# Expert blocks of a mixture of experts: one pass for a wide block and a block of 32 rows together, each piece of code once behind a branch

## Chip, core and metric

One core of a Trainium2 chip runs the whole kernel in one launch. The metric is the time of one execution in microseconds of the device; of several executions, the median.

## What is computed

A graph network's two attention layers, then one transformer block whose feed-forward part is a mixture of experts, on 625 rows of 768 numbers, all in float32. The change touches the last part alone:

```python
h2 = _ln(x, ln2_g, ln2_b).reshape(-1, d)              # 625 x 768
gate_logits = h2 @ Wg                                 # 8 experts
w, sel = jax.lax.top_k(gate_logits, 1)
...
hid = jax.nn.relu(jnp.einsum('nd,edf->enf', h2, W1) + b1[:, None, :])   # 768 -> 3072
y = jnp.einsum('enf,efd->end', hid, W2) + b2[:, None, :]                # 3072 -> 768
return x + moe.reshape(b, t, d)      # each row takes the y of its one expert
```

With one expert per row the softmax weight is 1, so a row's result is its sum `x` plus its expert's `y`. The experts' loads are uneven: the reference's gate sends 293, 152, 82, 57, 36 and 5 rows to six of them and none to two.

## The kernel before

Engines: PE (TensorE) multiplies, DVE (VectorE) and ACT (ScalarE) work on tiles, POOL (GpSimd) issues transfers by computed rows, SP (SyncE) issues all other transfers. Each engine runs its own queue in order. Inside the expert stage the orders of PE and of SP are written out by hand; a scheduler places the instructions of the others.

**Rows.** After the gate, each tile of 125 rows is scattered to HBM by expert, `xg` for the normalised rows and `xr` for the sums with the row's number behind them (`send`, `send_sums`, L998 to L1013). An expert has 640 places in both. Places that no row took hold a number beyond the last row, and a scatter to `out` leaves those out.

**The first expert.** The expert that has most of the first 125 rows is taken up while the other rows are still on their way: up to 128 of its rows are one pass ahead of the loop (`step_a`). Beside it DVE works out a table for the rest.

**The table** (L1330 to L1417). The rows left of each expert are cut into blocks of 128 rows, a block of 64 and a block of 32; each block is one pass of the loop, smaller blocks first. Each entry has the block's kind, its first row, its expert, whether the next pass's expert is a new one, and the same of the pass after that. `SHUFFLE` orders the experts by rank.

**One pass** (`step`, L1163 to L1275) holds the hidden rows as they come from the matmul, with rows on partitions:
- `into(c)` multiplies the turned rows `xbT` by a chunk of W1 into PSUM (L1186) and DVE copies it out (`hb`, L1190). With 64 or 32 rows, two or four chunks of columns share the array side by side.
- `turn(c)` transposes 128x128 pieces of `hb` on the PE (L1197), and ACT adds b1 and applies the relu on the way out (L1203).
- `out_of(c)` multiplies these by W2 into `py` (L1212).
- At the end DVE adds b2 and the row's sum (L1259, L1268), and POOL scatters the rows to `out` (L1270).

Within a pass, chunks of `into` and `out_of` follow closely. `turn_rows` (L905) transposes the next pass's rows `xb` on the PE in the last two chunks, and ACT copies them to `xbT`. POOL loads `xb` (L1456) and the sums `rb` (L1136), both 128 rows or less at 3 KB a row, and waits for what a pass before left in those tiles.

**Weights.** W1 and W2 of one expert fill six pieces in SBUF, three of 3 MB each. SP refills a piece for the next expert as soon as the last matmul that reads it is done (`load_expert`, L1144), each piece in two halves. The third piece of W1 has a copy ahead: `load_ahead` fills two spare tiles with that of the expert after next, and ACT copies them into place in each pass (`from_ahead`, L1161).

**The loop** (L1450 to L1470) reads the table entry on every engine and branches to one of three bodies, each a whole `step` with its loads:

```python
with tc.If(kind == 0) as cmp:
    part(B)
with cmp.Else():
    with tc.If(kind == 1) as cmp2:
        part(64)
    with cmp2.Else():
        part(32)
```

Of the kernel before, what the change touches and what calls it, by code (L numbers as in the profile page):

```python
# [20 lines left out]
N = 625  # L21
# [21 lines left out]
NS = E * 2 + N // B  # L43
SHUFFLE = (0, 3, 1, 4, 2, 5, 6, 7)
TA = 3
RE = 640
NR = E * RE + B
# [3 lines left out]
BH = E * NK // 2  # L51
NEG = -1.0e30
# [10 lines left out]
def gnn_moe_kernel(ctx: ExitStack, tc: tile.TileContext, p, out):  # L63
# [630 lines left out]
    with tc.tile_pool(name="att", bufs=1, reuse_waits="tile") as a1, \  # L694
# [210 lines left out]
        def turn_rows(dst, src, ps, part, copy):  # L905

            k0, k1 = ((0, 4), (4, KD))[part]
            tp = ps.tile([128, 512], F32, tag="tp", name="tpx").rearrange("p (k r) -> p k r", k=4)
            for k in range(k0, k1):
                nc.tensor.transpose(tp[:, k - k0, :], src[:, k * 128:(k + 1) * 128], ident)  # L910
            return copy(dst[:, k0:k1, :], tp[:, :k1 - k0, :])
# [86 lines left out]
        def send(t):  # L998

            pk = ps.tile([128, 512], F32, tag="tp", name="pk")  # L1000
            for s in range(t + 1):
# [5 lines left out]
                                           op0=OP.mult, op1=OP.add, accum_out=slot)  # L1007
            nc.vector.scalar_tensor_tensor(pos[t], ef[:, t:t + 1], float(RE), slot, op0=OP.mult,
# [70 lines left out]
        nc.gpsimd.dma_start(xa, xg[ds(first_e * RE, B), :])  # L1079
# [6 lines left out]
        nc.gpsimd.dma_start(ra, xr[ds(first_e * RE, B), :])  # L1086
# [17 lines left out]
    def load_half(to, e, c, k, **cond):  # L1104
        nc.sync.dma_start(to, W1[ds(e, 1), k * 128:(k + 3) * 128, c * FC:(c + 1) * FC]
                          .rearrange("o (k p) f -> p (o k) f", p=128), **cond)

    def load_piece(e, l, c, **cond):
        if l:
# [4 lines left out]
            for i in range(2):  # L1114
                nc.sync.dma_start(to[i], of_e[i], **cond)  # L1115
# [9 lines left out]
    ps = ctx.enter_context(tc.tile_pool(name="rps", bufs=1, space=PSUM, reuse_waits="tile"))  # L1125
    sp = ctx.enter_context(tc.tile_pool(name="sps", bufs=2, space=PSUM, reuse_waits="tile"))
    piece(ewa, 0, 0)
# [6 lines left out]
    def sums_so_far(row, M):  # L1134
        rb = mw.tile([B, D + 1], F32, name="rb", bufs=1)
        nc.gpsimd.dma_start(rb[:M], xr[ds(row, M), :])  # L1136
        return rb
# [6 lines left out]
    def load_expert(e, new, later, last=NFC - 1):  # L1144


        with tc.manual_schedule(engines={SP}):
            for c in range(last):
                load_piece(e, 0, c, cond=new)
            load_bias(e, cond=new)  # L1150
            load_piece(e, 1, 0, cond=new)
            load_ahead(*later)
            for c in range(1, NFC):
                load_piece(e, 1, c, cond=new)

    def load_ahead(e, new=None):
        for i in range(2):
            load_half(ahead[i], e, NFC - 1, 3 * i, **({} if new is None else dict(cond=new)))

    def from_ahead(i):  # L1160
        nc.scalar.copy(w1[NFC - 1][:, 3 * i:3 * i + 3, :], ahead[i])  # L1161

    def step(M, xT, bT, rb, after=None):  # L1163

        P = B // M
        C = 512 if P == 1 else FC // P
        n = DF // (C * P)
        K = C // 128  # L1170
        py = [sp.tile([128, 512], F32, name=f"py{i}", bufs=1) for i in range(2)]
        hb, hbT, copied = {}, {}, []

        def block(c, g, k):

            return 2 * k + c % 2 if P == 1 else g * K + k

        def into(c):
# [5 lines left out]
            for k in range(KD):  # L1184
                for g in range(P):
                    mm = nc.tensor.matmul(  # L1186
                        ph[g * M:(g + 1) * M, :C].rearrange("p (j f) -> p j f", f=128),
                        xT[:, k, :M], w[:, k, g], start=(k == 0), stop=(k == KD - 1))
            hb[c] = mw.tile([128, 512], F32, name="hb")
            copied.append(nc.vector.tensor_copy(hb[c][:, :C], ph[:, :C]))  # L1190
            return mm

        def turn(c):

            tp = sp.tile([128, 4, 128], F32, tag="tp", name="tph")
            for k in range(K):
                nc.tensor.transpose(tp[:, k, :], hb[c][:, k * 128:(k + 1) * 128], ident)  # L1197
            hbT[c] = mw.tile([128, 4, 128], F32, name="hbT", bufs=6)
            for k in range(K):
                for g in range(P):  # L1200
                    f = block(c, g, k) + (c // 2 if P == 1 else c) * (FC // 128)
                    r = slice(g * M, (g + 1) * M)
                    nc.scalar.activation(hbT[c][:, k, r], tp[:, k, r], AF.Relu, bias=bT[:, f:f + 1])  # L1203

        def out_of(c):
            w = w2[c // 2 if P == 1 else c]

            order = [(k, i) for k in sorted(range(K), key=lambda k: block(c, 0, k) % 2)
                     for i in range(2)]
            for k, i in sorted(order, key=lambda o: o[1]) if c == n - 1 else order:  # L1210
                for g in range(P):
                    mm = nc.tensor.matmul(  # L1212
                        py[i][g * M:(g + 1) * M, :384], hbT[c][:, k, g * M:(g + 1) * M],
                        w[:, block(c, g, k), i * 384:(i + 1) * 384],
# [3 lines left out]
        with tc.manual_schedule(engines={PE}):  # L1218
            into(0)
            begun = into(1)  # L1220
        yield begun
        if after is None:
            with tc.manual_schedule(engines={PE}):
                turn(0)
                turn(1)
                yield out_of(0)
        with tc.manual_schedule(engines={PE}):
            if after is None:
                into(2)
                into(3)  # L1230
                turn(2)
                out_of(1)
                for c in range(2, n):
                    if c + 2 < n:
                        into(c + 2)
                    else:
# [265 lines left out]
```

## Time and profile before

| what | us |
|---|---|
| median of three runs (lowest, highest) | 1045.74 (1045.42, 1046.21) |
| the profiled execution, its own time | 1046.59 |
| its span, first to last instruction | 1045.0 |
| PE's first matmul in the loop, and the end of its last | 689.72, 1032.89 |
| one chunk of `into` or `out_of`: 128 rows, 64 rows, 32 rows | 5.15, 5.31, 2.73 |
| transposes of hidden rows per chunk: 128, 64, 32 rows | 0.44, 0.59, 0.37 |
| transposes of the next rows, two parts in a pass: 128 rows | 0.44 + 0.22 |
| the same, 64 or 32 rows | 0.44 + 0.37 |
| from 700 to 1045: PE, DVE, ACT busy, of 345 | 318.2, 55.8, 103.7 |
| one copy of `from_ahead` on ACT | 2.75 |
| DVE's copy of 128x512 out of PSUM, of 128x256 | 0.69, 0.43 |
| load of 32 sums from issue to landing, median; the shortest load of sums, in the first pass | 5.4, 3.5 |
| scatter to `out` from issue to landing: median; the last one | 5.6, 2.3 |

How to read it: "busy" counts an instruction's time on its engine. A line of the timeline gives start, length, engine, line of the source, operation, what it writes and reads with shapes (a matmul 128*64 has 64 rows), how many instructions were merged, and in brackets the idle time before them with what ended it. Each float32 matmul shows as two. In a line of stretches the last three figures are the granted clock of the PE (1.00 is full), the busy share of the 16 transfer engines and GB/s. "T" will be used for the end of a pass on the PE.

### The profile page before, as it was taken

To read this page: it belongs to the slowest core of one execution; us is meant where nothing else is said; L and a number is where in the kernel's file an instruction comes from. 1 tells how busy PE (TensorE), PEld (TensorE's weight loads), DVE (VectorE), ACT (ScalarE), POOL (GpSimd) and SP (SyncE) were. 2 spreads that over 40 slices of the span, in tenths; PEclk is the share of its full clock that TensorE was granted. 3 is DMA by queue.
4 is the path that set the end of the run, shared out by engine and by line. 5 is a ranking of instruction groups with operands and counts; after the bars stand their busy time and mean duration, and the time that the engine had idled before them with its cause. 6 is when DMAs were issued, how large, how long until landed. Compare 5 with 4: busy or idle time off the path is not lost. (4 is left out here: it accounts for less than half of the span.)

```text
span 1045.0 us, 14928 instructions
## 1 busy us (share of the span) xinstructions
PE 984.0 (94%) x4733; PEld 568.7 (54%) x4734; DVE 449.4 (43%) x1337; ACT 355.6 (34%) x791; POOL 57.0 (5%) x97
## 2 busy tenths in 40 slices
PE   6889999999999999999999899998999899999893
PEld 4455456677555556677776555543454344634241
DVE  7877697285375740475545545011101121011212
ACT  6667554263140120444442201113131243134232
POOL 1200100000000010000000112000000000000000
PEclk9999999999999999999999889999999999999997
DMA  9300400300230173999300778333759977899893
GB/s 287 137 1 2 163 31 0 136 1 1 74 77 1 46 182 70 392 383 353 132 1 1 276 259 317 122 118 135 267 220 393 404 292 263 319 397 399 313 403 131
DMA packets 86197, 195.93 MB, mean 187 GB/s; under 512 B 32429, under 2 KB 34100, under 8 KB 86137
## 3 DMA queue, kind: packets, MB, share of 16 engines
q1 hardware_dynamic: 80617, 177.14, 47.2%
q0 software_dynamic: 5440, 17.86, 5.1%
q8 instruction: 34, 0.56, 0.2%
q14 instruction: 26, 0.21, 0.1%
q10 hardware_dynamic: 80, 0.16, 0.1%
HBM read 253.45 MB, written 38.37 MB: 279 GB/s over the span
## 5 line engine op out<-in xcount | busy, mean ns | idle before, releaser
L1212 PE MATMUL py<-ew,hbT 128*64 128x384 f32 (+2 forms) x960 | 187.8, 498 | 6.8 <-DMA ew<-in_L_ffn_W_dram 6.8
L1186 PE MATMUL ph<-ew,xbT 128*32 128x256 f32 (+2 forms) x864 | 155.2, 498 | 9.3 <-issue 4.8
L1212 PEld LDWEIGHTS py<-ew,hbT 128*64 128x64 f32 (+2 forms) x960 | 88.9, 145 | 85.6 <-issue 51.0
L1203 ACT ACTIVATE hbT<-tph,bT 128x64 f32<-128x64 f32 (+2 forms) x240 | 55.2, 333 | 229.5 <-PE tph L1197 162.6
L1186 PEld LDWEIGHTS ph<-ew,xbT 128*32 128x32 f32 (+2 forms) x864 | 62.1, 136 | 92.3 <-issue 84.6
L1268 DVE TENSOR_TENSOR yo<-yo,py 64x192 f32<-64x192 f32 (+2 forms) x80 | 27.6, 378 | 158.5 <-PE py L1212 157.7
L1190 DVE COPY hb<-ph 128x512 f32<-128x512 f32 (+1 forms) x39 | 24.4, 629 | 159.9 <-PE ph L1186 159.9
L530 PE MATMUL agg<-xl,zT 125*125 125x256 f32 (+1 forms) x300 | 79.8, 417 | 1.3 <-ACT zT L519 1.1
L530 PEld LDWEIGHTS agg<-xl,zT 125*125 125x125 f32 x300 | 54.5, 188 | 19.6 <-ACT zT L519 2.6
L357 PE MATMUL pp<-w,yT 128*125 128x512 f32 x120 | 56.1, 607 | 0.0
L232 ACT ACTIVATE step<-iota,past 125x314 f16<-125x314 f16 x120 | 55.9, 549 | 0.0
L630 PE MATMUL ph<-wr,h1T 128*125 128x384 f32 x160 | 52.8, 486 | 0.0
L592 PE MATMUL ph<-w,h1T 128*125 128x384 f32 x160 | 52.4, 486 | 0.0
L249 PE MATMUL cps<-step,oh 125*125 125x314 f16 x181 | 37.1, 307 | 10.5 <-ACT step L232 5.4
L854 DVE CUSTOM_DVE_ANT_0 e<-sc,later 125x625 f32<-125x625 f32 (+4 forms) x60 | 29.8, 542 | 36.2 <-PE sc L838 36.2
L858 ACT ACTIVATE e<-e,of 125x625 f32<-125x625 f32 (+4 forms) x60 | 35.7, 596 | 23.3 <-DVE of L854 23.3
L920 PE MATMUL po<-wpj,aT 128*125 128x384 f32 x120 | 42.8, 504 | 0.4 <-DVE xx L924 0.4
L167 PE MATMUL ph<-wr,yT 128*125 128x512 f32 x96 | 42.1, 593 | 0.1
L242 DVE TENSOR_SCALAR oh<-iota,drel,upper 125x125 f16<-125x125 f16 x160 | 41.1, 315 | 2.3 <-PE cps L249 2.2
L592 PEld LDWEIGHTS ph<-w,h1T 128*125 128x125 f32 x160 | 30.0, 188 | 21.2 <-issue 0.5
L630 PEld LDWEIGHTS ph<-wr,h1T 128*125 128x125 f32 x160 | 29.8, 188 | 20.8
L772 PE MATMUL pv<-L_ffn_Wv,hT 128*125 128x384 f32 x120 | 39.5, 486 | 0.0
(337 smaller groups left out, 1253.6 us busy)
## 6 DMA issues: line engine op xcount, KB each, us to landing
ew<-in_L_ffn_W_dram SPq DMA_DIRECT2D x114, 1536.0 KB
xr<-zt SPq DMA_DIRECT2D x5, 3076.0 KB
xg<-zt SPq DMA_DIRECT2D x5, 3072.0 KB
ahead<-in_L_ffn_W_dram SPq DMA_DIRECT2D x10, 1536.0 KB
xid<-in_L_ffn_W_dram SPq DMA_DIRECT2D x10, 1536.0 KB
w<-in_L_gnn_W_dram SPq DMA_DIRECT2D x4, 1536.0 KB
wr<-in_L_gnn_Wr_dram SPq DMA_DIRECT2D x4, 1536.0 KB
b2b<-in_L_ffn_b_dram SPq DMA_DIRECT2D x11, 384.0 KB
```

Of the source, the lines that this page charges most:

```text
L167: nc.tensor.matmul(pp[:R, :], yT[:, c, cols(t)], part(wr1, KD, c, i, 512), start=(c == 0), stop=(c == KD - 1))
L232: nc.scalar.activation(o, iota[:, :SH + 1], AF.Sign, bias=at, scale=-1.0)
L242: m = nc.vector.tensor_scalar(o, iota[:, :n], at, weight, op0=OP.is_equal, op1=OP.mult)
L357: nc.tensor.matmul(pp[:R, :], yT[:, c, cols(t)], part(w1, KD, c, i, 512), start=(c == 0), stop=(c == KD - 1))
L530: nc.tensor.matmul(self.agg[:R, c0:c0 + n], zT[:, s, :], xl[:, s, x0:x0 + n], start=(s == 0), stop=(s == T - 1))
L592: nc.tensor.matmul(ph[:R, :384], h1T[:, c, cols(t)], part(w2, KH, c, i, 384), start=(c == 0), stop=(c == KH - 1))
L630: nc.tensor.matmul(ph[:R, :384], h1T[:, k, cols(t)], part(wr2, KH, k, i, 384), start=(k == 0), stop=(k == KH - 1))
L772: nc.tensor.matmul(pp[:R, :384], hT[:, c, cols(t)], w[i][:, c, :], start=(c == 0), stop=(c == KD - 1))
L920: nc.tensor.matmul(po[t, i][:R, :384], aT[:, c, cols(t)], wpj[i][:, c, :], start=(c == 0), stop=(c == KD - 1))
L1186: mm = nc.tensor.matmul(ph[g * M:(g + 1) * M, :C].rearrange("p (j f) -> p j f", f=128), xT[:, k, :M], w[:, k, g], start=(k == 0), stop=(k ...
L1203: nc.scalar.activation(hbT[c][:, k, r], tp[:, k, r], AF.Relu, bias=bT[:, f:f + 1])
L1212: mm = nc.tensor.matmul(py[i][g * M:(g + 1) * M, :384], hbT[c][:, k, g * M:(g + 1) * M], w[:, block(c, g, k), i * 384:(i + 1) * 384], star ...
```

## The change

**Passes.** A pass now takes at most one wide block (128 or 64 rows) and one block of 32, of the same expert; an expert with 160 rows left has one pass of 128+32. The entry has three bits for the pieces, the expert, the new flag and the same of the next pass. Rows for a pass are read as one run of 160 places, the block of 32 first; so each expert's places begin 32 later in `xg` and `xr`. The order of experts changes (`SHUFFLE`).

**Order in a pass.** All `into` chunks and part of the turns of the wide block (`begin`), then the narrow block as a whole, then the rest of the wide block (`end`). W1 for the next expert is asked for after the narrow block's first matmuls (or after `begin`), W2 after `end`. The copy of W1 ahead is gone.

**Transposes.** DVE turns the next rows in blocks of 32x32 with one instruction. For this POOL loads `xb` as four quarters of the columns, 32 partitions each, 160 rows in runs of 192 numbers, and W1 lies in SBUF with rows 6p to 6p+5 of it on partition p. `xb` and its turned form take the place of `xid`, so the first expert's rows are still turned on the PE. The narrow block's hidden rows are turned by DVE too, straight from PSUM, and ACT applies bias and relu in place; its matmuls read W1 in runs of 32 columns.

**Scatters.** Each pass sends both: the wide block's rows, then the narrow block's. A block that a pass does not have has all its row numbers set beyond the last row.

The core of the diff:

```diff
-NS = E * 2 + N // B
-SHUFFLE = (0, 3, 1, 4, 2, 5, 6, 7)
+NS = E + N // B
+SHUFFLE = (0, 3, 2, 4, 1, 5, 6, 7)
+Q = 32
+U = B // Q + 1
...
+            nc.vector.tensor_scalar_add(slot, slot, float(Q))
...
-        nc.sync.dma_start(to, W1[ds(e, 1), k * 128:(k + 3) * 128, c * FC:(c + 1) * FC]
-                          .rearrange("o (k p) f -> p (o k) f", p=128), **cond)
+        nc.sync.dma_start(to, W1[ds(e, 1), :, c * FC:(c + 1) * FC]
+                          .rearrange("o (p k) f -> p (o k) f", p=128)[:, k:k + 3], **cond)
...
-    def load_ahead(e, new=None):
-        for i in range(2):
-            load_half(ahead[i], e, NFC - 1, 3 * i, **({} if new is None else dict(cond=new)))
-
-    def from_ahead(i):
-        nc.scalar.copy(w1[NFC - 1][:, 3 * i:3 * i + 3, :], ahead[i])
...
+    def load_first(e, new):
+        with tc.manual_schedule(engines={SP}):
+            for c in range(NFC):
+                load_piece(e, 0, c, cond=new)
+
+    def load_second(e, new):
+        with tc.manual_schedule(engines={SP}):
+            load_bias(e, cond=new)
+            for c in range(NFC):
+                load_piece(e, 1, c, cond=new)
...
+        def begin(self):
+            self.into(0)
+            self.into(1)
+            for c in range(2, self.n):
+                self.turn(c - 2)
+                mm = self.into(c)
+            return mm
+
+        def end(self):
+            n = self.n
+            self.out_of(0)
+            self.turn(n - 2)
+            self.turn(n - 1)
+            for c in range(1, n):
+                mm = self.out_of(c)
+            return mm
+
+    def prepare(rows, idx, M):
+        nc.vector.tensor_copy(idx[:M], rows.bitcast(I32)[:M, D:D + 1])
+        nc.vector.tensor_add(rows[:M, :D], rows[:M, :D], b2b[:M])
...
+    w1b = ewb.tile([128, 2, KD, FC], F32, name="w1b")
+    w1[1:] = [w1b[:, i] for i in range(2)]
...
+    def rows_in(row):
+        rows = xg[ds(row, U * Q), :].rearrange("(b r) (q c) -> q r b c", r=Q, q=4)
+        for q in range(4):
+            nc.gpsimd.dma_start(xb[q * Q:(q + 1) * Q], rows[q])
+
+    def turn_next():
+        return nc.vector.transpose(xT.rearrange("p j (b r) -> p b j r", r=Q),
+                                   xb.rearrange("p b (r j) -> p b j r", r=Q))
...
+    def narrow(bT, *then):
+        def into(c, n, w):
+            ph = sp.tile([128, 512], F32, name="ph")
+            v = ph[:, :n * BLK * Q].rearrange("p (c j r) -> p c j r", c=n, r=Q)
+            for k in range(KD):
+                for g in range(4):
+                    nc.tensor.matmul(v[g * Q:(g + 1) * Q], xT[:, k, :Q], w[:, :, k, :, g],
+                                     start=(k == 0), stop=(k == KD - 1))
+            to = hq[:, c * BLK:(c + n) * BLK]
+            nc.vector.transpose(to, ph[:, :n * BLK * Q].rearrange("p (j r) -> p j r", r=Q))
+            for j in range(c * BLK, (c + n) * BLK):
+                nc.scalar.activation(hq[:, j, :], hq[:, j, :], AF.Relu, bias=bT[:, j:j + 1])
...
+            into(0, 1, w1[0][:, None].rearrange("p c k (j g r) -> p c k j g r", g=4, r=Q))
+            into(1, 2, w1b.rearrange("p c k (j g r) -> p c k j g r", g=4, r=Q))
+        load_first(*then)
...
+                        nc.tensor.matmul(
+                            pq[i][g * Q:(g + 1) * Q, :384], hq[:, c * BLK + j + g, :],
...
+        prepare(rq, iq, Q)
+        add_up(rq, pq, Q)
...
+        rows_in(row_next)
+        nc.gpsimd.dma_start(rw, xr[ds(row + Q, B), :])
+        nc.gpsimd.dma_start(rq, xr[ds(row, Q), :])
+        bT, s = biases((w >> 8) & 7)
...
+        with tc.If((w & 2) == 2) as c64:
+            with tc.manual_schedule(engines={PE}):
+                of[64].begin()
+        with c64.Else():
+            with tc.If((w & 4) == 4):
+                with tc.manual_schedule(engines={PE}):
+                    of[B].begin()
+        with tc.If((w & 1) == 1) as c32:
+            narrow(bT, *then)
+        with c32.Else():
+            nc.vector.memset(iq, N)
+            load_first(*then)
+        turn_next()
+
+        def finish(M):
+            if M < B:
+                nc.vector.memset(iw[M:], N)
+            prepare(rw, iw, M)
+            with tc.manual_schedule(engines={PE}):
+                of[M].end()
+            load_second(*then)
+            add_up(rw, pw, M)
+
+        with tc.If((w & 2) == 2) as d64:
+            finish(64)
+        with d64.Else():
+            with tc.If((w & 4) == 4) as d128:
+                finish(B)
+            with d128.Else():
+                load_second(*then)
+                nc.vector.memset(iw, N)
+        for rows, idx, M, after in ((rw, iw, B, first_made), (rq, iq, Q, first_load)):
+            s = scatter_out(rows, idx, M)
+            tc.add_manual_dep(s.ins, after.ins.name, ORDER)
```

`rq`, `iq`, `pq` and `hq` are the narrow block's sums, row numbers, results in PSUM and hidden rows; `rw`, `iw` and `pw` the wide block's. `add_up` adds the results in PSUM to the sums as the old lines L1262 to L1268 did; `Wide.into`, `turn` and `out_of` do what the old functions of these names did.

## The prediction

> **What bounds the kernel now.** I read the page first, then its stretches, then the PE's work in order of time over the expert stage, last the queue of POOL.
>
> ```profile
> span 1045.0 us, 14928 instructions
> ...
> PE 984.0 (94%) x4733; PEld 568.7 (54%) x4734; DVE 449.4 (43%) x1337; ACT 355.6 (34%) x791; POOL 57.0 (5%) x97
> ```
>
> TensorE bounds the span. The change lies in the loop over experts, from 689.7 us on, and in how it is entered. The PE's matmuls there, some of them (start, length, what they are, idle time before):
>
> ```profile
> 727.12 11.98 PE L1186 MATMUL ph<-ew,xbT 128*128 128x512 f32 x24 [3.07 <-DVE bT L1142]
> ...
> 833.02 6.75 PE L1186 MATMUL ph<-ew,xbT 128*32 128x256 f32 x96 [4.82 <-issue]
> ...
> 852.50 10.57 PE L1186 MATMUL ph<-ew,xbT 128*128 128x512 f32 x24
> ...
> 917.85 10.52 PE L1186 MATMUL ph<-ew,xbT 128*64 128x512 f32 x48
> ...
> 952.10 5.39 PE L1186 MATMUL ph<-ew,xbT 128*32 128x256 f32 x96
> ...
> 971.35 3.12 PE L1212 MATMUL py<-ew,hbT 128*32 128x384 f32 x24 [2.91 <-DMA ew<-in_L_ffn_W_dram]
> 974.39 11.19 PE L1186 MATMUL ph<-ew,xbT 128*64 128x512 f32 x48
> ...
> 1009.32 5.39 PE L1186 MATMUL ph<-ew,xbT 128*32 128x256 f32 x96
> ...
> 1029.58 3.31 PE L1212 MATMUL py<-ew,hbT 128*32 128x384 f32 x24 [2.99 <-DMA ew<-in_L_ffn_W_dram]
> ```
>
> The reader is to see nine passes, of 64, 128, 64, 32, 128, 64, 32, 64 and 32 rows, and that most begin without a gap. An undisturbed pass takes 917.85 - 852.50 = 65.35 us (128 rows) or 952.10 - 917.85 = 34.25 (64); one of 32 is 18.2 from its pieces in the table above. Two 128, four 64 and three 32 make 322.3; the PE works until 1032.9, 343.2 after 689.7. The other 20.9: **first visits** to the body for 128 rows (3.07, and 11.98 - 10.57 = 1.4 at a lower clock) and for 32 rows (4.82, and 6.75 - 5.39), together 10.7; **weights** that came late in the seventh and ninth pass (22.3 and 23.6 us instead of 18.2, and 0.7 at 974.39), together 10.2.
>
> **The change, part by part.**
>
> *Passes.* By the new table the same blocks make seven passes: 64 | 128 | 64 | 64+32 | 64 | 128+32 | 32. The matmuls that stream weights stay. Gone from the PE: the rows' turn (0.81 in the four passes of 64 and the three of 32, 0.66 in the two of 128, 0.66 in the first pass), 7.7; the turn of the hidden rows in the blocks of 32, three of 0.37 each in three blocks, 3.3. **-11.0.** VectorE takes them: a turn of 960 columns, by the copy of 512 at 691 ns some 1.3 us, in a stage where it is busy 56 of 345 us. The PE does not wait for it before the next pass: it stands behind the first matmuls and has 17 us (64 rows) or more of second matmuls as cover. The new 32-row matmuls read W1 in runs of 32 columns, not 128; no row shows that: bounds 0 and, were they twice as slow, three times 8.1 us. I take 0, since the old pass of 128 rows reads W1 in runs of 128 columns and that of 64 in one run of 512, and their matmuls take 605 and 600 ns. ScalarE loses eighteen copies of 2.75 us that ended no wait.
>
> *First visits.* The old loop has one body for each width; the new one has five pieces (start 64, start 128, narrow, end 64, end 128) in the order in which they run. Of the old bodies the first cost what the loop's entry shows in both; the other two cost 10.7. Bounds: all hidden (-10.7), or four new pieces at 5.3 each (+10.7). I take **0**. The row that bears on it: the last packet of the instruction queue lies at 828 us, and the five later jumps between bodies (852, 917, 952, 974, 1009) leave no gap.
>
> [...]
>
> *Weights.* The rows of 3 MB read ahead go; instead the first matmuls of a pass all end before its second ones, so that W1 of the next expert can be loaded during the second half, and W2 during the next first half. The queue carries about 400 GB/s when full:
>
> ```profile
> 940.00:950.00 10.00, 10.00 (x64) 4.76 (x64) 0.34 (x2) 2.59 (x10) 0.00 (x0) 1.00 1.03 405
> ```
>
> So 3.95 us per half piece of 1.57 MB, 48.5 for an expert with its bias, and about 4 for the rows, sums and results of a pass (1.4 MB, much of it now in runs of 768 bytes). From the start of the third pass the queue is full: 8 (the last W2 of its own expert), two experts 97, one pass's rows three times 12, the first W1 piece of the sixth pass 8 and 1.5 to land: 126.5. The PE wants it after 33.5 + 49.8 + 33.5, with 2.6 of slack and about 3 of a first visit: 122.4. It waits 4, some 5 with the piece behind it, and no longer in the last pass: 5 - 10.2 = **-5**. Bounds: -10.2 (rows cost 2.5) and +8 (rows 6, halves 4.2). If a chain of transfers this full slips, every us is the PE's.
>
> *A new wait in the last pass.* In the build's order of instructions VectorE's first two in the narrow piece are the index copy and the addition of b2 to rq (942 ns in the old row for 32 rows), both behind the load of rq; the turns of the narrow hidden rows are queued behind them, ScalarE's relus behind these, and the PE's second matmuls behind those. The load of rq is the last of POOL's six loads, and POOL now sends two scatters per pass, the second only when the first has landed. POOL's rows (start, length), a 128-row pass that ended on the PE at 793.96, and the last:
>
> ```profile
> 795.66 1.02 POOL L1270 DMA_INDIRECT out_dram<-yo,idx  x1 [64.50 <-DVE yo L1268]
> 798.84 0.58 POOL L1456 DMA_DIRECT2D xb<-xg  x1 [2.15 <-PE ph L1186]
> 800.06 0.54 POOL L1136 DMA_DIRECT2D rb<-xr  x1 [0.65 <-issue]
> ...
> 1036.79 0.92 POOL L1270 DMA_INDIRECT out_dram<-yo,idx  x1 [19.94 <-DVE yo L1268]
> ```
>
> and the time from issue to landing, medians, last in each line:
>
> ```profile
> rb<-xr POOLq DMA_DIRECT2D x3, 96.1 KB, 5.4
> out_dram<-yo,idx POOLq DMA_INDIRECT x10, 5.6
> ```
>
> With T the end of a pass on the PE: first scatter T+1.7, landed T+7.3, second scatter out T+8.3, first rows 2.15 later, T+10.5; four issues of 0.57 with gaps of 0.65 to T+15.4; rw to T+16.6; rq landed between 3.5 (its shortest, quiet queue) and 5.4 later, T+21. Then 0.14 + 0.94, the turn of 256 columns 0.43, a relu 0.30: the PE goes on at T+22.8. In the pass 64+32 its first matmuls end at T+24.4, in 128+32 far later: hidden. In the last pass, 32 rows alone, they end at T+8.1: 14.7 lost, of which a slower landing or gaps could make 18 and faster ones 10. A low clock after it (3.31 us for the last 24 matmuls) is inside that spread. **+15.**
>
> *The end.* After VectorE's last addition there stand now, before the scatter that counts: the turn for a pass that does not come (1.3), two branches and a memset (0.5, the old loop's turn-round of 1.4 at most), and the wide scatter, all of it out of bounds, which must land first: 0.97 (its issue) to 5.6; the shortest in the old trace, the quiet last one, took 2.3, to which I hold. With a little for the second hand-over, **+4.5**, bounds 2.5 to 8.
>
> [...]
>
> *Small ones, at nothing:* one more addition on 125x1 per tile; the order in which the first expert's W2[1] and W1[2] are released swaps, so W1[2] lands by my count near 654 to 656 and its halves are wanted at 655.3 and 657.9 (bounds 0, +2).
>
> Sum: -11.0 + 0 - 5 + 15 + 4.5 = +3.5, on the profiled execution's 1046.6 (span 1045.0 and 1.6 around it) 1050.1. That execution lies 0.85 above the median of the runs, so **1049** on their scale. A measurement of this kernel can tell about 0.2%, 2.1 us, from no change.
>
> **Rivals.**
> (a) *Faster: the code is found ready.* The five pieces lie in order of execution, so that fetching ahead may cover their first visits. Then -10.7: 1038. For it: the old gaps follow jumps backward or over a body. Against: the 4.82 has no visible cause. It decides from 5.5 us of the 10.7 saved.
> (b) *Faster: the last pass waits little*, since POOL's queue turns faster than its old rows: at a wait of 3 us, 1037. Against: each step is a row.
> (c) *Slower still: the full queue.* Row packets or the new address order of W1 cost more: halves at 4.2 and rows at 6 make the +8 above, 13 more than forecast: 1062.
> (d) *The terms cancel* to within 2.1 us.
> (e) *Every jump stalls:* two in each of seven passes at the 3.07 us of 727.12 are 43 us: 1092. Against: the five jumps without a gap.
>
> **Chances.** Forecast, 1047.9 to 1056: 0.34; (c) 0.12; (e) 0.03; so slower 0.49. (a) 0.21 and (b) 0.14: faster 0.35. (d) 0.16. The range 1036 to 1063 takes in all but the ends of (b), (c) and (e); the forecast's own is 1048 to 1056.
>
> **What will show it.** Right: no transposes on the PE in the loop but those of the wide blocks; seven passes; in the last, an idle PE of 10 to 18 us between first and second matmuls that VectorE's rq addition ends; two scatters at the end, 2 to 6 us apart; waits for weights only about the sixth pass. Wrong: gaps at every branch, DMA below 380 GB/s in the full stretch, or a last pass without the wait.

## The result, and the profile after

The changed kernel took 1053.41 us (median of four runs, 1051.67 to 1054.71) against 1045.58 of the kernel before in the same runs: ratio 1.0075, 95% interval 1.0058 to 1.0093. The forecast was 1049, slower, within 1036 to 1063, a range that also takes in faster times. The sign held, and so did the narrower range of the forecast itself, 1048 to 1056; the loss, 7.8, is more than twice the 3.3 forecast. The profiled execution took 1053.03 us, 6.44 more than that of before. The head of its page:

```profile
span 1049.5 us, 14689 instructions
...
PE 974.1 (93%) x4511; PEld 597.8 (57%) x4512; DVE 462.8 (44%) x1347; ACT 301.0 (29%) x753; POOL 78.4 (7%) x129
```

TensorE is busy 9.9 us less than before (984.0), and the time is longer all the same: what was taken off the engine that bounds the kernel came back as time in which it stands still. PE's matmuls in the loop at three of the six seams, at the waits for weights and in the last pass (start, length, what they are, idle time before; PEq and DVEq are the queue of an engine, its branches and waits, and not the engine itself):

```profile
708.27 5.49 PE L1213 MATMUL pw<-ew,hT 128*64 128x384 f32 x32 [0.68 <-PEq L1513]
...
759.49 5.40 PE L1213 MATMUL pw<-ew,hT 128*128 128x384 f32 x16 [1.01 <-DVE hb L1190]
...
843.13 2.80 PE L1460 MATMUL ph<-ew,xid 128*32 128x256 f32 x48 [1.02 <-DVE hb L1190]
...
909.53 4.09 PE L1213 MATMUL pw<-ew,hT 128*64 128x384 f32 x24 [1.83 <-DMA ew<-in_L_ffn_W_dram]
...
917.21 7.96 PE L1187 MATMUL ph<-ew,xid 128*128 128x512 f32 x18 [0.82 <-DMA ew<-in_L_ffn_W_dram]
...
962.51 2.98 PE L1476 MATMUL pq<-ew,hq 128*32 128x384 f32 x30 [0.30 <-DMA ew<-in_L_ffn_W_dram]
...
1000.64 4.36 PE L1460 MATMUL ph<-ew,xid 128*32 128x256 f32 x48 [3.11 <-DVEq L1510]
1004.81 5.34 PE L1460 MATMUL ph<-w1b,xid 128*32 128x512 f32 x48
1018.70 11.00 PE L1476 MATMUL pq<-ew,hq 128*32 128x384 f32 x96 [8.55 <-issue]
```

The first matmul of the second to the sixth pass does not wait. There are three kinds of gaps: one of 0.7 to 1.0 us inside every pass with a wide block, at the seam between its two halves; three short waits for weights about the sixth pass; and two long ones in the last pass. The label "issue" of the longest says only that the profile saw no single releaser. VectorE's rows of the same time show what it was (start, length, operation, idle time before):

```profile
1016.63 0.14 DVE L1238 COPY iq<-rq 32x1 int32<-32x1 int32 x1 [17.08 <-DMA rq<-xr]
1016.86 0.94 DVE L1239 TENSOR_TENSOR rq<-rq,b2b 32x768 f32<-32x768 f32 x1
1017.73 1.03 DVE L1463 STREAM_TRANSPOSE hq<-ph 128x256 f32<-128x256 f32 x2
```

VectorE stood 17.08 us at the load of rq, and the turns of the hidden rows, whose input was there from 1005 on, were queued behind it, as forecast. GpSimd's rows about that time and at the end:

```profile
999.25 1.05 POOL L1254 DMA_INDIRECT out_dram<-rw,iw  x1 [68.98 <-DVE rw L1250]
1006.54 0.90 POOL L1254 DMA_INDIRECT out_dram<-rq,iq  x1 [6.24 <-DMA out_dram<-rw,iw]
1009.73 2.65 POOL L1435 DMA_DIRECT2D xid<-xg  x4 [2.29 <-issue]
...
1013.66 0.54 POOL L1501 DMA_DIRECT2D rq<-xr  x1 [0.40 <-issue]
1036.04 1.05 POOL L1254 DMA_INDIRECT out_dram<-rw,iw  x1 [21.84 <-DVE iw L1536]
1039.04 0.90 POOL L1254 DMA_INDIRECT out_dram<-rq,iq  x1 [1.96 <-DMA out_dram<-rw,iw]
```

The second scatter waits 6.24 for the first one's landing, and the load of rq is the last of six: it went out 16.1 after TensorE had ended its pass at 997.5. The stretches of 10 us show the clock (last three figures: granted clock, busy share of the transfer engines, GB/s):

```profile
1000.00:1010.00 10.00, 9.36 (x96) 3.87 (x96) 0.00 (x0) 0.00 (x0) 1.47 (x3) 0.83 0.92 361
1010.00:1020.00 10.00, 1.45 (x13) 1.18 (x13) 2.04 (x4) 1.72 (x9) 3.23 (x6) 0.70 0.32 100
1020.00:1030.00 10.00, 9.70 (x93) 8.46 (x85) 1.48 (x3) 3.48 (x17) 0.00 (x0) 0.78 0.00 0
```

The clock was half for 3.4 us from 1000.4 and for 10.2 us from 1014.1. The first matmuls of the pass took 4.36 instead of 2.80, the last ones 11.00 instead of 8.52: 4.0 us more behind gaps of 11.7.

From the two profiled executions, the difference by its parts:

| part | how | forecast | measured |
|---|---|---|---|
| matmuls and turns themselves | 338.5 from 691.18 to 1029.70, less the 24.8 of gaps and low clock below = 313.7; before 322.3 | -11.0 | -8.6 |
| first visits, seams | the 10.7 of before are gone; six seams: 0.84, 1.01, 0.82, 1.75, 0.81, 0.98 = 6.2 | 0 | -4.5 |
| waits for weights | 1.83 + 0.82 + 0.30 = 2.95; before 10.2 | -5 | -7.2 |
| the last pass | 8.55 + 3.11 + clock 4.0 | +15 | +15.7 |
| from TensorE's end to the span's | 19.8 (1029.7 to 1049.5); before 12.1 (1032.9 to 1045.0) | +4.5 | +7.7 |
| the loop's start | 691.18; before 689.72 | 0 | +1.5 |
| outside the span | 3.53; before 1.59 | none | +1.9 |
| sum | | +3.5 | +6.4 |

### The profile page after: what moved, and what is told of

It reads as the page before. It is cut to its first block, busy times and chain, and to the rows that moved or that the text cites. A ratio compares the mean times of both kernels' runs of the same rounds, so it can differ in the third digit from the quotient of the medians.

```text
span 1049.5 us, 14689 instructions
## 1 busy us (share of the span) xinstructions
PE 974.1 (93%) x4511; PEld 597.8 (57%) x4512; DVE 462.8 (44%) x1347; ACT 301.0 (29%) x753; POOL 78.4 (7%) x129
## 5 line engine op out<-in xcount | busy, mean ns | idle before, releaser
L1213 PE MATMUL pw<-ew,hT 128*64 128x384 f32 (+1 forms) x672 | 159.8, 487 | 5.5 <-PEq L1513 2.0
L1213 PEld LDWEIGHTS pw<-ew,hT 128*64 128x64 f32 (+1 forms) x672 | 101.4, 160 | 58.3 <-issue 14.1
L1203 ACT ACTIVATE hT<-tph,bT 128x64 f32<-128x64 f32 (+1 forms) x168 | 41.0, 361 | 282.6 <-PE tph L1198 188.5
L1187 PE MATMUL ph<-w1b,xid 128*64 128x512 f32 (+1 forms) x288 | 85.7, 594 | 0.0
L1190 DVE COPY hb<-ph 128x512 f32<-128x512 f32 x30 | 20.7, 691 | 142.0 <-PE ph L1187 142.0
L1187 PEld LDWEIGHTS ph<-w1b,xid 128*64 128x64 f32 (+1 forms) x288 | 34.5, 155 | 41.5 <-issue 37.7
L1250 DVE TENSOR_TENSOR rw<-rw,pw 64x192 f32<-64x192 f32 (+1 forms) x48 | 12.9, 315 | 92.5 <-PE pw L1213 92.3
L1187 PE MATMUL ph<-ew,xid 128*64 128x512 f32 (+1 forms) x144 | 43.1, 595 | 1.8 <-SPq L1493 1.0
```

The source lines that it names most:

```text
L1187: mm = nc.tensor.matmul(ph[g * M:(g + 1) * M, :C].rearrange("p (j f) -> p j f", f=128), self.xT[:, k, :], w[:, k, g], start=(k == 0), stop ...
L1203: self.made = nc.scalar.activation(hT[c][:, k, r], tp[:, k, r], AF.Relu, bias=self.bT[:, f:f + 1])
L1213: mm = nc.tensor.matmul(pw[i][g * M:(g + 1) * M, :384], hT[c][:, k, g * M:(g + 1) * M], w[:, self.block(c, g, k), i * 384:(i + 1) * 384], ...
```

## The experiments

Three theories were at stake. For the last pass: VectorE's queue at rq's load, set by GpSimd's queue, or else the weights. For the seams: the hand-over of the last copy, the skipped branch, or code that has to be fetched. For the end: the second scatter, or something behind it. Single runs of one kernel lie up to 10 us apart here (1039.2 to 1049.4 of the kernel before), while its medians were 1044.5 to 1045.6 in the groups of runs; so ratios are compared, and single gaps in the traces.

**1. The work on rq behind the turns.**

```diff
-        prepare(rq, iq, Q)
+        with tc.issue_after(turned.ins):      # the last turn of the hidden rows
+            prepare(rq, iq, Q)
         add_up(rq, pq, Q)
```

> The changed kernel with one thing moved: in the narrow block VectorE turns the hidden rows first, and only then copies rq's row numbers and adds b2. Theory (VectorE's queue): the 8.55 us that TensorE idles in the last pass between first and second matmuls are VectorE standing at the load of rq (landed at 1016.6) with the turns queued behind it. Then the idle time falls to about 1 us (a turn 0.43, a relu 0.32, hand-overs), and the half clock that followed it (second matmuls 11.0 us instead of 8.5) goes as well: 8.55 - 1 + 2.5 = 10 less, 1043. Rival (weights): TensorE waits for W2, whose last pieces were on their way until about 1008; then the idle time stays near 8 and the time at 1053. Rival (the wait moves): the additions of the results wait for rq instead, at the end of the pass; they start at about 1021 and rq lands at 1016.6, so I expect nothing of it.

Measured 1042.82, ratio 0.9963 (0.9944 to 0.9981). The wait is gone:

```profile
1000.89 4.49 PE L1460 MATMUL ph<-ew,xid 128*32 128x256 f32 x48 [3.10 <-DVEq L1512]
1005.17 5.36 PE L1460 MATMUL ph<-w1b,xid 128*32 128x512 f32 x48
1010.32 7.95 PE L1477 MATMUL pq<-ew,hq 128*32 128x384 f32 x96
```

VectorE still waited for rq, until 1017.06, but with nothing behind it that TensorE needs. The queue theory holds with its size, 10.6 of forecast 10. This one order of two instructions is more than the whole loss: without it the change makes the kernel faster by 0.4%.

**2. The scatters independent of each other.**

```diff
+        tc.declare_no_dep(both[1].ins, both[0].ins, reason="other rows")
```

> The changed kernel with the two scatters of a pass declared to touch different rows, so that the second does not wait until the first has landed; the scatter of the narrow rows then stands ahead of the wide one in GpSimd's queue. Theory (GpSimd's queue sets when rq is loaded): in the pass before the last, 6.24 us of waiting for a landing and an issue of 0.9 go from in front of the last pass's loads, so rq lands 7 us earlier, TensorE's idle time falls from 8.55 to about 1.5 and the half clock after it mostly goes (-2.5); at the end the second scatter no longer waits 1.96 for the first, -3. Together 12 less: 1041. Rival (the load of rq is bound by the weights in the transfer queues): it lands no earlier, only the end gains: 1050.5.

Measured 1047.60, ratio 1.0014 (0.9991 to 1.0036): between the two. GpSimd asked for rq at 1007.91, 5.7 earlier, but its transfer, as the view of transfers shows (last column: us from issue to landing), took 7.2; in the changed kernel it took 2.9:

```profile
rq<-xr POOLq DMA_DIRECT2D x1, 96.1 KB, 7.2
```

```profile
rq<-xr POOLq DMA_DIRECT2D x1, 96.1 KB, 2.9
```

The weights' transfers were under way until 1015.5 here (1010.4 in the changed kernel), and rq's rows shared the transfer engines with them, which were 90% busy or more until 1012. So rq landed only 1.4 earlier: GpSimd's queue bounds the load in the changed kernel, and once that queue is shorter the transfers do. The wait fell from 8.55 to 6.42, and the way from the last addition to the end of the span by 3.0.

**3. The seam filled with 5 us of matmuls.**

```diff
                 mm = self.into(c)
+            self.out_of(0)
             return mm
         def end(self):
             n = self.n
-            self.out_of(0)
```

> The changed kernel with the first chunk of second matmuls (5 us on TensorE) moved from behind the seam between the two halves of a wide block to ahead of it; nothing else changes. Theory (hand-over): the gaps of 0.66 to 1.02 at the six seams are TensorE waiting for VectorE's last copy out of PSUM (0.69) and for the branches, with nothing queued; with 5 us of matmuls that need neither, five or six of them go, 4.5 to 6 less in all: 1048. Rival (the jump itself costs: code has to be fetched): a gap stays at each seam, the time stays within 1 us of 1053.4.

Measured 1054.07, ratio 1.0076 (1.0052 to 1.0100): nothing gained. In the four passes without a narrow block the gap moved along with the seam, and behind it came a second one, since the turns now stand first there. The third pass:

```profile
815.50 1.06 PE L1198 MATMUL tph<-ident,hb 128*128 128x128 f32 x8 [0.69 <-PEq L1513]
816.97 10.64 PE L1213 MATMUL pw<-ew,hT 128*64 128x384 f32 x64 [0.41 <-ACT hT L1203]
```

So there it is not the copy. In the two passes with a narrow block, where the branch is taken, the gaps of 1.02 and 0.98 ahead of its matmuls are gone: there it was the wait for the copy. The trace has the steps of PE's queue: at the narrow block's branch not taken, it waits until its own matmuls under way are done and adds to their count what the skipped ones would have added; then come a branch and some four steps of 0.1 us each before the next matmul. In the changed kernel's first pass the last matmul ended at 707.59, the step stands at 707.66, the branch at 707.81 and the next matmul at 708.27. The kernel before has no such step inside its loop.

**4. The kernel before, its bodies laid out in the order of their first use** (64, 128, 32 rows):

```diff
-        with tc.If(kind == 0) as cmp:
-            part(B)
+        with tc.If(kind == 1) as cmp:
+            part(64)
         with cmp.Else():
-            with tc.If(kind == 1) as cmp2:
-                part(64)
+            with tc.If(kind == 0) as cmp2:
+                part(B)
```

> The kernel before, with the three bodies of its loop laid out in the order in which the passes first come to them: 64, 128, 32 rows instead of 128, 64, 32. Nothing else changes. Theory (code is fetched ahead in the order of memory): the gaps at the first visits, 3.07 and 4.82, with the lower clock behind each (1.4 and 1.36), come from jumping to code that the fetch had not reached; the jump to 32 rows at least now falls through into the next body, so 6 to 9 us go: 1037 to 1040. Rival (the first run of any body costs that, wherever it lies): the gaps stay, 1045.6. Rival (the 3.07 is VectorE's last additions and its way through the loop's turn, since the trace names VectorE's bias copy as what ended it): only the 6.2 of the body for 32 rows go, 1039.5.

Measured 1047.08, ratio 1.0014 (0.9996 to 1.0031): no gain, and yet the gap at the first pass of 32 rows is gone, as the theory had it. It turned up elsewhere:

```profile
727.79 12.23 PE L1186 MATMUL ph<-ew,xbT 128*128 128x512 f32 x24 [4.64 <-issue]
...
797.26 10.52 PE L1186 MATMUL ph<-ew,xbT 128*64 128x512 f32 x48 [2.39 <-DVE bT L1142]
...
831.51 5.39 PE L1186 MATMUL ph<-ew,xbT 128*32 128x256 f32 x96
```

In the trace there stands in each of these gaps the end of one long branch instruction of PE: 5.73 and 6.00 us here, 4.36 and 5.93 in the kernel before, where others take 0.1 to 0.4. While each of the four lasts, at least one packet of 16 KB starts in the instruction queue (at 721.4 and 792.9 here, at 722.7 and 828.3 before). Here they are the jumps from the end of the 64-row body over the two others, and from that of 128 over the last one; in the kernel before, the jump from the 64-row body over that for 32, in the first pass and again in the third. So the stall belongs to these four jumps, not to the body that is visited first. In all four the body right behind the jump had not run. Where that one had run and only a further one had not (788.43 in the kernel before, 828.21 here), the jump took 0.2. The theory of a first visit falls; that of code which has to be fetched is neither refuted nor shown, as no run sets it apart from everything else that comes with a jump. The changed kernel has one such branch in its loop, 3.50 us at 703.53 of the first pass, where the narrow block is skipped for the first time. It lies under matmuls that were already issued, and the gap behind it is 0.68 like those of the later seams. After that pass no branch takes over 0.5 us. The instruction queue between 760 and 830, of the kernel before, where the changed kernel has no such line:

```profile
q8 instruction: 3, 0.05, 0.3%
```

**5. One more branch not taken, in the midst of matmuls.**

```diff
+            with tc.If((w & 2048) == 2048):
+                with tc.manual_schedule(engines={PE}):
+                    nc.tensor.transpose(tp[:, 0, :], hb[0][:, :128], ident)
```

> The changed kernel with a branch that is never taken put into the second half of a wide block, between its second and third chunk; it holds one transpose on TensorE. The seam of the changed kernel sits where VectorE's last copy is also awaited, this one in the midst of matmuls that wait for nothing. Theory (a skipped branch drains TensorE): at a branch with TensorE work that is not taken, TensorE's queue waits for its own matmuls under way before it steps their count, as the trace shows at the four passes without a narrow block (gaps of 0.66, 0.67, 0.68 and 1.01); then each of the six passes with a wide block loses another 0.6 to 0.8: 1057 to 1058. Rival (the gaps are VectorE's copy and the jump's own 0.2): at most 0.2 a pass, 1053.4 to 1054.6. A side effect: some requests for W2 come later, which can add a us or two to the waits for weights; the gaps themselves are read from the trace.

Measured 1052.88, ratio 1.0077 (1.0050 to 1.0105); the profiled span 1050.9, 1.4 more than that of the changed kernel. The added branch shows as a gap of 0.28 in the four passes with 64 rows (the releaser named is not the one) and as none in those of 128. The second matmuls of the first pass, in the changed kernel and here:

```profile
714.94 10.69 PE L1213 MATMUL pw<-ew,hT 128*64 128x384 f32 x64 [0.16 <-issue]
```

```profile
715.19 2.12 PE L1213 MATMUL pw<-ew,hT 128*64 128x384 f32 x10 [0.15 <-issue]
717.59 9.24 PE L1213 MATMUL pw<-ew,hT 128*64 128x384 f32 x54 [0.28 <-ACT hT L1203]
```

The gap is not the whole price: the same 64 matmuls take 11.64 from first to last instead of 10.69. Measured from the first turns of one pass to those of the next, three of the four passes with 64 rows are 0.95 longer and those of 128 rows 0.4 (the fourth of 64 can't be compared, as it has waits for weights in the changed kernel). By an estimate from these, 4.6 in six passes: the theory's 0.6 to 0.8 a pass holds in sum. The time did not rise all the same, since the waits for weights fell from 2.95 to 0.25 and the time outside the span from 3.5 to 1.7.

**6. The row loads issued by ScalarE.**

```diff
-            nc.gpsimd.dma_start(xb[q * Q:(q + 1) * Q], rows[q])
+            nc.scalar.dma_start(xb[q * Q:(q + 1) * Q], rows[q])
```

> The changed kernel with the four quarter loads of the next rows issued from ScalarE's queue instead of GpSimd's; GpSimd then issues as many transfers as in the kernel before (57 instead of 89). Theory (transfers issued by GpSimd cost at the end): GpSimd's last instruction, which waits until its queue is drained, took 8.3 us in the changed kernel and 5.7 in the one before, and the time outside the span was 3.5 instead of 1.6; with 57 transfers both return: 2.6 and 1.9 less. Besides, the load of rq is issued 3 us earlier; in the run with free scatters 5.7 us earlier brought 1.4, the weights being in the way, so I expect 1 of it. Together 5.5 less: 1048. Rival (the drain hangs on the number of scatters, which stays, or on the shape of the loop): the end stays as it is, 1052.

Measured 1077.86, ratio 1.0317 (1.0291 to 1.0342): 25 us slower, by something I had not priced here. In ScalarE's queue the loads stand ahead of the relus, and from the fourth pass on they were held until 20 to 30 us into a pass; TensorE waited for the relus behind them. PE's row, then ScalarE's:

```profile
964.89 1.12 PE L1198 MATMUL tph<-ident,hb 128*128 128x128 f32 x4 [12.56 <-ACT hT L1203]
```

```profile
963.70 2.17 ACT L1203 ACTIVATE hT<-tph,bT 128x128 f32<-128x128 f32 x8 [40.77 <-DMA xid<-xg]
```

What held the loads is in the trace: ScalarE's queue waits for a semaphore, a counter that a transfer steps when it lands, and weights that SyncE asked for step the same one. The load ahead of the row above waits for semaphore 140, which a transfer of W2, asked for at 940.83, steps until 960.77; the wait ends at 960.79. The two passes before show the same (855.08 and 855.10, 907.52 and 907.54). In the changed kernel the row loads have semaphores of their own. The question asked was answered nevertheless. GpSimd's long instruction at the end, which drains its queue, and the number of transfers GpSimd issued, over all runs:

| transfers by GpSimd | last drain, us | kernels |
|---|---|---|
| 57 | 5.70 to 5.83 | before, experiments 4, 6, 8 |
| 83 | 7.83, 7.95 | 9, 10 |
| 89 | 8.31 to 8.46 | after, 1, 2, 3, 5, 7, 11, 12 |

Each transfer costs (8.32 - 5.71) / 32 = 0.08 us in that drain. The time outside the span did not follow (3.5 with 57 transfers).

**7 and 8. Three places mended; the same with the loads by ScalarE.** The edits of 1 and 2, and `turn_next()` ahead of `prepare(rq, iq, Q)` where there is a narrow block.

> The changed kernel with three of its places mended: VectorE turns the narrow hidden rows ahead of the work on rq (1042.8 by itself), the two scatters don't wait for each other, and in a pass with a narrow block VectorE turns the next rows before it touches rq, not after the additions. Theory (terms at the end add up): 1.96 of waiting for a landing and the issue behind it, 3.0 together, and the turn, 1.87, which is then done while VectorE waits for rq; since the memset and GpSimd's way to the wide scatter come in their place, 3.5 less than with the first alone: 1039, 0.6% under the kernel before. Rival (the last scatter's way is set by something else, the drain above all): 1042.8.

> The one before it with the row loads issued from ScalarE's queue as well. Theory: another 4.5 less at the end (2.6 drain, 1.9 outside the span): 1034.5. Rival (the drain hangs on the scatters): as without, 1039. Rival (ScalarE's relus wait behind the loads that wait for room): slower than without, 1041 or more.

Measured 1040.91, ratio 0.9967 (0.9946 to 0.9988), and 1066.72, ratio 1.0209 (1.0182 to 1.0236). In 8 ScalarE's queue again sets the time, as a rival there had it, though the loads wait for the semaphore and not for room. In 7 the end is shorter as expected: 13.0 from the last addition to the end of the span, 16.4 in experiment 1. GpSimd's last two rows stand close together now:

```profile
1019.19 0.91 POOL L1254 DMA_INDIRECT out_dram<-rq,iq  x1 [15.72 <-DVE iw L1540]
1020.62 1.04 POOL L1254 DMA_INDIRECT out_dram<-rw,iw  x1 [0.51 <-issue]
```

By the ratios, though, 7 can't be told from 1. One reason may be seen in its trace: behind the start of the sixth pass there are waits for weights of 1.29 and 1.69, where the changed kernel has 0.30. But the execution profiled took 1035.0, 5.9 less than the median.

**9, 10, 11. Without the load of rw in each pass,** from the changed kernel and from that of 7, and 7 again beside them. Kernels 9 and 10 leave out the sums and row numbers of the wide blocks of later passes; they serve for the time alone:

```diff
+    nc.gpsimd.dma_start(rw, xr[ds(row_0 + Q, B), :])      # once, ahead of the loop
...
-        nc.gpsimd.dma_start(rw, xr[ds(row + Q, B), :])
```

> The changed kernel without the load of the wide block's sums in each pass: rw is loaded once, ahead of the loop, so the sums and row numbers of the wide blocks are left out. That takes 385 KB from the transfer queues per pass, 0.95 us at 405 GB/s. Theory (the queues are full from the third pass on, so every us of other traffic is TensorE's): the waits for weights in the fifth pass and behind it (1.83, 0.82 and 0.30) come after three or four such loads and fall to under 0.5 together: 2.5 less; six transfers fewer in the last drain and an earlier load of rq give another 0.5 to 1.5: 1049 to 1050.5. Rival (the weights are late because the room for them comes free late, and the queues have slack): the waits stay, 1052 to 1053.

> The kernel with the three places mended, and the same load left out. In that kernel the waits for weights were 2.25, 0.81, 1.29 and 1.69, 6.0 together, against 2.95 in the changed kernel: what it won at the end it seems to have lost here. Theory (full queues): they fall to 2 or less, and the time by 4 to 5 against the run beside it. Rival (room comes free late): no more than 1 less.

> The kernel with the three places mended once more, as the measure for the run without the load of rw on the same chip: 1041, 0.3% under the kernel before.

Measured 1046.40, ratio 1.0004 (0.9987 to 1.0022); 1035.12, ratio 0.9900 (0.9872 to 0.9928); 1039.73, ratio 0.9957 (0.9937 to 0.9978). The single waits differ between two executions of one kernel (those behind the sixth pass's start are 0.51 in 11). The time until a given point of the loop varies less. From the loop's first matmul to the one in the sixth pass that waits for W1 (917.21 in the changed kernel) it took 226.0 us there, 226.2 in 7 and 226.2 in 11; without the load 223.0 in 9 and 223.6 in 10. PE's rows shortly before that point, of 11 and of 10:

```profile
910.68 4.09 PE L1213 MATMUL pw<-ew,hT 128*64 128x384 f32 x24 [1.62 <-DMA ew<-in_L_ffn_W_dram]
```

```profile
905.06 4.09 PE L1213 MATMUL pw<-ew,hT 128*64 128x384 f32 x24 [0.62 <-DMA ew<-in_L_ffn_W_dram]
```

So 2.6 to 3.0 went, what three loads at 0.95 take: the queues are full (from 850 to 1000 the transfer engines show a share of 1.03 and 389 to 405 GB/s in 9), and other traffic there was TensorE's time. The wait of 0.8 at the start of the sixth pass stays in all of them. The rest of 9's gain lies behind that point (3.3 until TensorE's end, of it 2.1 in the last pass), in the drain (0.5) and in the spread; my 2.5 to 4 was too little.

**12. The first expert's W1 ahead of its W2,** on the kernel of 7:

```diff
-    for l, c in ((0, 1), (1, 1), (0, 2), (1, 2)):
+    for l, c in ((0, 1), (0, 2), (1, 1), (1, 2)):
```

> The kernel with the three places mended, and the third piece of the first expert's W1 requested ahead of the second piece of its W2. In the changed kernel the two stood the other way round: W2's piece was requested at 632.6 (in the kernel before at 615.5), W1's behind it, and TensorE waited for W1 at 658.5, 3.54 us; in the kernel before the same matmuls did not wait for weights, and the loop began 1.46 earlier. Theory (order of requests): W1's piece lands 8 us earlier, before 655, W2's near 660, where its first matmul runs at 674; the wait goes, and the loop begins 1.5 to 3 us earlier: 1037.5 on the scale on which the same kernel without this took 1039.7, 0.6% under the kernel before. Rival (weights in the loop are behind by as much, so what is won here is waited for there): 1039 to 1040.

Measured 1033.84, ratio 0.9889 (0.9863 to 0.9915): 5.9 less than 11, more than expected. The wait for W1 before the loop, 3.6 in 11, is gone, and with it a stretch of 3.4 us at half clock behind it, in which six matmuls took 4.54 in 11 instead of 2.74; the loop begins at 686.99 instead of 692.13, though TensorE was level with 11 at 637. A part is waited for later: 2.08, 2.20 and 1.74 for weights. This is the best version: 1.1% under the kernel before and, by their ratios, 1.8% under the changed one.

## Why the prediction was right, and where it was not

- **Sign and place: right; the sum in part by luck.** The last pass, 15.7 of forecast 15, is what makes the change a loss, by the mechanism named; experiment 1 shows it by taking it away. The rest of the sum came near only because its errors have both signs: first visits and weights cost 6.7 less than forecast, the other terms 9.7 more. The last pass's make-up was off, too. The load of rq came at T+19.1, not T+21 (it landed in 2.9, in queues that had run empty), and the first matmuls began 3.1 late, for a reason I had not seen: a narrow block alone waits until VectorE has ended the last additions of the pass before, turned its loop and walked past the branches not taken (the releaser, DVE's queue at L1510). And 4.0 are the clock, which I had put inside the spread. The late start costs nothing by itself, as the wait for rq covers it: TensorE went on at T+21.2, 1.6 ahead of the forecast, and the half clock behind that took 2.5 more.
- **The end: half right.** 9.3 from TensorE's end to the last scatter instead of 3.9 is 5.4, 0.9 over the 4.5 forecast; 0.6 of that is the turn for the pass that does not come, which took 1.9 and not 1.3. Behind the last scatter stand another 2.2, from a drain that is 2.6 longer. The step that failed is the count of what 32 more transfers by GpSimd cost: I priced their issue and landing, not the drain.
- **First visits: the value failed, the bounds held.** I took 0 for gone and added; the 10.7 are all gone, as rival (a) had it, though not because all code was found ready: one jump of the first pass still stalled for 3.50, under cover of matmuls. The new cost is the seams, 6.2, that no rival named at this size. Rival (e), 3.07 at every jump, is refuted. The stalls of 4.4 to 6.0 us stand at two jumps each of the kernel before and of experiment 4, with a packet of the instruction queue starting while each lasts; the jumps of the later passes, in both kernels, show no such packet and no stall. What makes a jump stall was not shown.
- **Weights: right in direction.** 2.95 at the sixth pass, forecast 5. Experiments 9 and 10 show that the queue is full up to there. What of the 7.2 comes from the new order of requests and what from the dropped copy ahead was not tried apart.
- **Transposes: 8.6 of 11.0.** Without their gaps the passes of 64 rows take 33.3 to 33.9 (33.5 worked out), and that of 64+32 takes 49.7 (49.8). Of the 2.4 missing, 0.7 are turns of the first pass, ahead of the loop, which the forecast counts and this row does not. Another 1.3 lie in the fifth and sixth passes, whose matmuls are broken by the waits for weights. The runs of 32 columns cost nothing: the narrow block's first 48 matmuls take 2.80, as before.
- **At nothing, wrongly:** the loop's start, +1.5. The swap of two requests, which I had bounded by 2, brought a wait of 3.54 by itself; the net is smaller because TensorE came there 1.2 earlier, and a wait of 1.62 and the turns of the kernel before are gone. Experiment 12 shows the swap to be worth more than its wait, through the clock.
- **Not in the sum at all:** 1.9 outside the span. It goes along with the instruction queue at the program's very end. Kernels with one packet or none of queue 14 there (before, 4; 5) have 1.6 to 1.7 outside their profiled spans, those with two to four have 3.4 to 4.1. The packets after 1040, of the kernel before and of the changed one:

```profile
q14 instruction: 1, 0.01, 0.1%
```

```profile
q14 instruction: 2, 0.02, 0.3%
```

It may be a matter of where the last code happens to lie; no experiment was made for it, and the cause stays open.

## What to carry to other kernels

Work that leaves the bounding engine for another engine's queue must be looked at there in its order: what stands ahead of it, and what that waits for. An instruction that waits for a transfer belongs behind everything that does not; here that order was worth 10.6 us, more than all that the change took off TensorE. A wait of some 3 us can cost twice, once as a gap and once as slow matmuls (3.1 and 1.6 in the last pass of the changed kernel).

## What the runs showed of the hardware

- **A gap of 3.1 us is followed by a lower clock in some executions and not in others.** The same gap at the start of the last pass was followed by matmuls of 4.33 to 4.49 us in the changed kernel and in experiments 1, 2, 9 and 11, and of 2.80 in 3, 5, 7, 10 and 12; 7 and 11 are one kernel. In the kernel before and the changed one, the stretches at half clock that end ahead of TensorE's last matmul are 3.4 us long or a multiple of that (6.8, 10.2). What decides whether the clock falls was not shown.
- **GpSimd's last drain was longer by 0.08 us for each further transfer that GpSimd issued** in the program: 5.71 us with 57 in the kernel before, 8.32 with 89 in the changed one.
- **A branch not taken that holds TensorE's work let TensorE run dry** in passes of 64 rows: a gap of 0.28 us in the midst of matmuls (experiment 5), but 0.95 by the stretch that it stands in; a gap of 0.67 with another branch behind it (the seams of the changed kernel).
- **Transfers waited for others that they had nothing to do with**: row loads that had a semaphore in common with weights were held until those had landed (20 to 30 us into three passes of experiment 6).
